# A pre-activation convolution on one core: the half sums m1 and m2 in a tile each

## The chip, the cores and the metric

The kernel runs on one core of a Trainium2 chip. The metric is device time in microseconds (us); the time before is the median of three runs, 1009.18 us (1008.23 to 1009.91). The engines are named as the profile names them: PE (matmuls), PEld (loading of PE's weights), DVE (vector), ACT (scalar), POOL, and SP, which issues transfers.

## The reference

There are 160 images of 128 channels and 32 x 32 pixels, and five weight sets. Each image is normalised in groups of four channels, convolved with the 3 x 3 weights of its set (128 to 128 channels, quantised to two levels first), and the image itself is added.

```python
w = (v1 + v2).reshape(OUT_CH * N, IN_CH, K, K)          # quantised U, N = 5
xb = x.reshape(B // N, N * C, H, W)
act = conv_general_dilated(xb, w, padding=[(1, 1), (1, 1)], feature_group_count=N)
g = v.reshape(B_, 32, C_ // 32, H_, W_)                  # _gn
return ((g - mean(g)) / sqrt(var(g) + 1e-5)).reshape(v.shape)
x = x + conv(_gn(x), U)
```

## The kernel before

Channels lie on the 128 partitions. `Main.run` goes over the 160 images set by set, 32 images for each of five weight sets. The order of the instructions on every engine is written out by hand in that loop, under a manual schedule: nothing is moved by a planner, and each engine works through its own list in order. Waits between engines are set where one engine writes a tile that another reads or overwrites; they go by tile.

**Two precisions.** Every normalised image is split into a float16 part and a float16 remainder, and the product of both with the weights is summed in PSUM. An image is either *direct* or *combined* (L524 to L529): up to image 145 every odd image from 7 on is combined and every even one direct; from image 146 on two of three are combined. For a direct image ACT makes `z` (L513) and `hi` (L521), DVE the remainder `lo` (L579) and its three combinations of rows: the differences (L593), the sums of row pairs (L595) and their differences (L596), all in the tile `rows`. For a combined image POOL and DVE combine the raw image's rows first (`v`: L544, L545, and L555, L558, L561), ACT rounds to `vh` (L566), DVE makes the remainder `vl` (L572).

**The half sums.** The convolution over three rows of taps saves work: for each pair of output rows two half sums are made, m1 and m2, from the sum and the difference of the two input rows, and the pair is m1 + m2 and m1 - m2. They live in the tile `m` (`self.pair`, L380), one PSUM bank for m1 and one for m2. The steps for image i are:

- `sums_of_pairs(i)` (L668, matmuls at L655): PE writes m2's bank first and then m1's. A combined image takes 12 matmuls, 6 for each; a direct one 6, 3 for each. A full one has 512 columns.
- `leave(i)` (L713): ACT copies m2 from PSUM to SBUF.
- `pairs(i)` (L723, L725): DVE writes m1 + m2 and m1 - m2 into the two banks of a tile `eo`, of which there are two. Between the two instructions the caller may put one more step (`between`).
- `rest_of_column(i)` (L619, L655): PE adds the remaining products into `eo`: 24 matmuls of 256 columns for a combined image; 18 of 512 and 12 of 256 for a direct one.
- `residual(i)` (L739): ACT halves `eo` into `sum`, and `accumulate(i)` (L752) adds it to the image with a DMA from POOL's queue. For the first three images and the last four, DVE does this itself (L744). `store` and `load` (L757, L409) are issued on SP.

**The order.** `conv(i)` issues the sums of image i + 1 first and then the rest of image i. In the same iteration DVE makes the remainder of image i + 2, then the pairs of i + 1, then `combine(i + 4)`. ACT does the residual of i - 1, leaves i + 1, and makes the parts of i + 3. Around these ACT takes the statistics of images further ahead: a sum (L192) and a sum of squares (L199) for nearly every image, up to 14 images ahead, until there are no images left, at about iteration 145. Steps that quantise the weights of the next set (the iterator `later`) are strewn between DVE's work. For a direct image i + 2 two of the combinations come before the pairs, and the third comes between the addition and the subtraction:

```python
self.low_part(i + 2)
take(later, 1)
rows = self.combinations(i + 2)
take(rows, 2)
...
self.pairs(i + 1, lambda: take(rows if i % 2 == 0 else later, 1))
run(rows)
```

Image 2, one of the first three, uses the two banks of `m` as its `eo`; L744 reads both in one instruction.

Of the kernel before, what the change touches and what calls it, by code (L numbers as in the profile page):

```python
# [309 lines left out]
class Main:  # L310
# [36 lines left out]
    def __init__(self, tc, ctx, keep, x, u, out):  # L347
        nc = self.nc = tc.nc
        self.imgs, C, self.H, self.W = x.shape
        P = self.P = nc.NUM_PARTITIONS  # L350
        assert C == P and self.H * self.W == 1024
        self.per_set = self.imgs // N_SETS
        self.xv = x.rearrange("(b n) c h w -> n c b (h w)", n=N_SETS)
        self.ov = out.rearrange("(b n) c h w -> n c b (h w)", n=N_SETS)
        self.uv = u.rearrange("n (o i k) -> n o i k", o=C, k=TAPS)

        def pool(name, bufs, **kw):
            return ctx.enter_context(tc.tile_pool(name=name, bufs=bufs, **kw))

        self.const = pool("const", 1)  # L360
        self.qpool = pool("quant", 1)
        self.wpool = pool("weights", 2)
        self.upool = pool("u", 1)
        self.xpool = pool("x", 11)
        self.zpool = pool("z", 3)
        self.parts = pool("parts", 5)
        self.rows = pool("rows", 4)
        self.wide = pool("wide", 2)
        self.wide_parts = pool("wide_parts", 3)
        self.evac = pool("evac", 2)  # L370
        self.sums = pool("sums", 3)
        self.unread = pool("unread", 1)
        self.small = pool("small", 3)
        self.ps_eo = pool("ps_eo", 2, space=PSUM)
        self.ps_m = pool("ps_m", 1, space=PSUM)
        self.ps_stat = pool("ps_stat", 1, space=PSUM)
        self.ps_tr = pool("ps_tr", 1, space=PSUM)
        self.steps = Steps(nc, keep)

        self.pair = self.ps_m.tile([P, 2, self.H // 2, self.W], F32, tag="m", name="m")  # L380
        self.chunks, self.z, self.hi, self.v, self.eo, self.m2 = {}, {}, {}, {}, {}, {}
        self.sum = {}
        self.wts = {}
        self.columns = []

        cuts = [0, 2, 4, 8, 12, 16, 20, *range(24, self.imgs + 1, 8)]
        self.groups = [range(a, b) for a, b in zip(cuts, cuts[1:])]
        self.group_of = {i: k for k, g in enumerate(self.groups) for i in g}
        self.stats = {}
# [215 lines left out]
    def taps(self, i, part, col, target, last, halves=(0, 1)):  # L605


        nc, H, W = self.nc, self.H, self.W
        tile, top = part
        n, _ = self.place(i)  # L610
        dw = col - 1
        c0, c1 = max(0, -dw), W - max(0, dw)
        for k in (1, 0, 2):
            for h in halves:

                h0 = h * (H // 2)
                r0, r1 = max(h0, 1 - k), min(h0 + H // 2, H + 1 - k)
                s0 = r0 + k - 1 + top
                nc.tensor.matmul(  # L619
                    target[:, h, r0 - h0 : r1 - h0, c0:c1],  # L620
                    self.wts[n, col][:, k, :],
                    tile[:, s0 : s0 + r1 - r0, c0 + dw : c1 + dw],
                    start=(i < self.FIRST and col == self.COLS[0] and k == 1 and top == 0),
                    stop=(last and k == 2),
                    skip_group_check=True,
                )

    def bank_pair(self, i):
        return self.ps_eo.tile([self.P, 2, self.H // 2, self.W], F32, tag="eo", name=f"eo{i}")

    def warm_up(self, count):


        zeros = self.los[3].rearrange("p h w -> p (h w)")
        for _ in range(count):
            self.nc.tensor.matmul(
                self.pair[:, 0].rearrange("p i w -> p (i w)"), zeros[:, :128],
                zeros[:, :512], start=True, stop=True,
            )

# [26 lines left out]

    def sums_of_pairs(self, i):  # L668

        m = self.pair  # L670
        both = self.both(i)
        for a, kind in ((1, self.DIFF), (0, self.SUM)):
            for col in self.COLS:
                for j, (_, st) in enumerate(both):
                    self.product(
                        m[:, a], i, kind, st[:, a], col,
                        col == self.COLS[0] and j == 0,
                        col == self.COLS[-1] and j == len(both) - 1,
                    )
# [30 lines left out]
    def leave(self, i):  # L710

        m2 = self.evac.tile([self.P, self.H // 2, self.W], F32, tag="m2", name=f"m2_{i}")
        self.nc.scalar.copy(m2, self.pair[:, 1])  # L713
        self.m2[i] = m2

    def pairs(self, i, between=lambda: None):


        nc = self.nc
        m1, m2 = self.pair[:, 0], self.m2.pop(i)  # L720
        eo = self.eo[i] = self.bank_pair(i)
        rows = eo.rearrange("p h (i a) w -> p (h i) a w", a=2)
        nc.vector.tensor_add(rows[:, :, 0], m1, m2)  # L723
        between()
        nc.vector.tensor_sub(rows[:, :, 1], m1, m2)  # L725
# [5 lines left out]
    def residual(self, i):  # L731

        nc = self.nc
        eo = self.eo.pop(i).rearrange("p h r w -> p (h r w)")
        del self.hi[i]
        n, b = self.place(i)
        if not self.by_hand(i):
            self.sum[i] = self.sums.tile([self.P, 1024], F32, tag="sum", name=f"sum{i}")
            nc.scalar.mul(self.sum[i], eo, 0.5)  # L739
            return  # L740
        xj = self.image(i)
        halves = [slice(0, 512), slice(512, 1024)] if i == self.imgs - 1 else [slice(0, 1024)]
        for h in halves:
            nc.vector.scalar_tensor_tensor(  # L744
                xj[:, h], eo[:, h], 0.5, xj[:, h], ALU.mult, ALU.add
            )
            if i >= self.imgs - LAST:
                nc.sync.dma_start(self.ov[n, :, b, h], xj[:, h])
# [12 lines left out]
    def run(self):  # L761
# [39 lines left out]
        def take(steps, count):  # L801
            for _ in range(count):
                next(steps, None)
# [73 lines left out]
        for i in range(self.imgs):  # L877
# [41 lines left out]
            if i < self.FIRST:  # L919

                if i == 0:
                    measure(0, 8, 9, 10)
                    self.normalise(4)
                    self.high_part(4)
                if i == 2:
                    self.leave(3)
                    self.normalise(5)
                    measure(1, 9)
                    self.high_part(5)
                    self.pairs(3)  # L930
                    self.low_part(4)
                    run(self.combinations(4))
                self.residual(j)
                if i == 1:
                    measure(0, 11)
            else:

                rows = iter(())
                if self.combined(i + 2):
                    self.low_combined(i + 2)  # L940
                elif i + 2 < self.imgs:
                    self.low_part(i + 2)
                    take(later, 1)
                    rows = self.combinations(i + 2)
                    take(rows, 2)
                if i > self.FIRST and self.by_hand(j):
                    self.residual(j)
                for k in by_scalar:
                    self.measure(k, (0,))
                if i > self.FIRST and not self.by_hand(j):  # L950
                    self.residual(j)
                    self.accumulate(j)
                if self.combined(i + 4):
                    self.outer_rows(i + 4)


                part = i + 3 < self.imgs and not self.combined(i + 3)
                if i + 1 < self.imgs:
                    self.leave(i + 1)
                if part:  # L960
                    self.normalise(i + 3)
                    self.high_part(i + 3)
                if self.combined(i + 3):
                    self.high_combined(i + 3)
                for k in by_scalar:
                    self.measure(k, (1,))
# [9 lines left out]
            if i >= self.FIRST:  # L976

                if i + 1 < self.imgs:
                    self.pairs(i + 1, lambda: take(rows if i % 2 == 0 else later, 1))
                run(rows)  # L980
                if self.combined(i + 4):
                    self.combine(i + 4)
                else:
                    take(later, 1)
                if b == self.per_set - 4:
                    run(later)
# [61 lines left out]
```

## Time and profile before

| what | value |
|---|---|
| median of three runs | 1009.18 us (1008.23 to 1009.91) |
| profiled execution, its own time | 1011.2 us |
| its span, first to last instruction | 1009.5 us |
| granted PE clock | 0.999 |
| busy PE, DVE, ACT, POOL | 960.5, 902.2, 912.1, 416.2 us |
| DMA moved | 254.42 MB, 252 GB/s on average |

The first part of the page gives the busy time of each engine as a share of the span. The table of windows gives it by stage, for stretches counted from the start of the span. In a group of instructions the busy time and the mean duration of one stand before the bar, and the time that the engine stood idle just before them behind it, with what ended it. In the list of waits a line names an engine and its line, what it waited for, the total in us, how often, and the longest. In the timeline a line is start, duration, engine, line, operation, what it writes and reads, and in brackets the idle time before it. A matmul's end in the trace is modelled: matmuls that follow one another overlap in the list.

### The profile page before, as it was taken

What the parts mean: (1) busy time and instruction counts of PE and PEld (TensorE: products, weight loads), DVE (VectorE), ACT (ScalarE), POOL (GpSimd) and SP (SyncE); (2) the same over time, 40 slices, a digit from 0 to 9 for tenths busy, and PEclk for the clock granted to TensorE, in tenths of its full rate; (3) what the DMA queues carried; (4) which work ended last, traced back from release to release, by engine and by line L of the source; (5) the groups of instructions that cost most, each with busy time, mean ns of one, the idle gap of its engine ahead of it and who ended that gap; (6) DMA issues with size and microseconds to landing.
All of it is one profiled execution on the core that took longest, in us unless ns stands there. A gap on an engine that the chain in (4) does not pass through costs nothing.

```text
span 1009.5 us, 15999 instructions
## 1 busy us (share of the span) xinstructions
PE 960.5 (95%) x5935; PEld 574.3 (57%) x5935; DVE 902.2 (89%) x1237; ACT 912.1 (90%) x1240; POOL 416.2 (41%) x581
## 2 busy tenths in 40 slices
PE   1999999999999999999999999999999999999996
PEld 0445555565556565665556566655565666655564
DVE  7999999998999999889999998998899988898884
ACT  4879999999999999999999999999999999997560
POOL 3535474553425262523434343427263723234220
PEclk9999999999999999999999999999999999999999
DMA  9529979999999999999999999998999999998664
GB/s 358 199 84 238 254 220 288 265 257 267 264 270 282 271 256 272 269 282 263 271 272 259 275 267 264 271 268 242 266 269 268 249 286 269 264 260 217 167 172 145
DMA packets 67287, 254.42 MB, mean 252 GB/s; under 512 B 5248, under 2 KB 5248, under 8 KB 67200
## 3 DMA queue, kind: packets, MB, share of 16 engines
q1 hardware_dynamic: 45168, 173.09, 50.6%
q0 software_dynamic: 22032, 80.23, 40.8%
q8 instruction: 48, 0.79, 0.3%
q14 instruction: 39, 0.32, 0.1%
HBM read 89.19 MB, written 83.89 MB: 171 GB/s over the span
## 4 chain that ended last, share of the span: by engine, by line
PE 55%; ACT 15%; DVE 11%; issue 6%; DMA 6%; POOL 6%; SPq 0%; POOLq 0%; ACTq 0%; DVEq 0%
PE m L655 19%; PE eo L619 19%; PE eo L655 15%; ACT junk L199 3%; DMA xt<-in_x_dram 3%; ACT vh L566 3%; DMA xt<-sum 2%; ACT m L713 2%; ACT sum L739 2%; DVE eo L723 2%; DVE eo L725 2%; ACT z L513 2%; DVE vl L572 1%; POOL rstd L235 1%; ACT junk L192 1%
## 5 line engine op out<-in xcount | busy, mean ns | idle before, releaser
L655 PEld LDWEIGHTS <-wt 128*128 128x128 f16 x4266 | 413.5, 98 | 255.8 <-DVE eo L725 25.0
L619 PE MATMUL eo<-hi,wt 128*128 128x496 f16 (+3 forms) x1422 | 339.7, 375 | 1.1 <-ACT wt L478 0.6
L752 POOL DMA_DIRECT2D xt<-sum x153 | 136.4, 895 | 425.7 <-ACT sum L739 409.2
L619 PEld LDWEIGHTS <-wt 128*128 128x128 f16 x1494 | 146.1, 99 | 143.0 <-ACT wt L478 1.8
L655 PE MATMUL m<-vh,wt 128*128 128x496 f16 (+1 forms) x480 | 182.7, 381 | 15.2 <-DVE eo L725 14.6
L572 DVE SCALAR_TENSOR_TENSOR vl<-v,rstd,vh 128x2048 f16<-128x2048 f32 x80 | 187.9, 2349 | 4.0 <-ACT vh L566 4.0
L655 PE MATMUL eo<-vh,wt 128*128 128x248 f16 (+1 forms) x960 | 184.0, 273 | 0.0
L655 PE MATMUL eo<-vl,wt 128*128 128x248 f16 (+1 forms) x960 | 184.0, 273 | 0.0
L655 PE MATMUL m<-vl,wt 128*128 128x496 f16 (+1 forms) x480 | 182.3, 380 | 0.0
L723 DVE TENSOR_TENSOR eo<-m,m 128x512 f32<-128x512 f32 x157 | 109.1, 695 | 80.2 <-ACT m L713 80.1
L192 ACT ACTIVATE junk<-xt 128x1024 f16<-128x1024 f32 x152 | 160.6, 1057 | 20.4 <-DMA xt<-in_x_dram 17.4
L199 ACT ACTIVATE junk<-xt,mv 128x1024 f16<-128x1024 f32 x152 | 174.0, 1145 | 0.2
L566 ACT ACTIVATE vh<-v,rstd 128x2048 f16<-128x2048 f32 x80 | 161.0, 2013 | 3.0 <-POOL v L545 2.0
L739 ACT ACTIVATE sum<-eo 128x1024 f32<-128x1024 f32 x153 | 154.0, 1006 | 8.2 <-PE eo L655 7.8
L655 PE MATMUL eo<-rows,wt 128*128 128x256 f16 (+1 forms) x924 | 139.0, 273 | 0.0
L713 ACT COPY m<-m 128x512 f32<-128x512 f32 x157 | 91.1, 580 | 38.9 <-PE m L655 36.2
L655 PE MATMUL m<-rows,wt 128*128 128x496 f16 (+1 forms) x462 | 112.5, 380 | 1.0 <-DVE rows L596 0.8
L725 DVE TENSOR_TENSOR eo<-m,m 128x512 f32<-128x512 f32 x157 | 108.5, 691 | 1.2
L513 ACT ACTIVATE z<-xt,shift,rstd 128x1024 f32<-128x1024 f32 x80 | 99.5, 1244 | 4.0 <-POOL shift L242 4.0
L579 DVE TENSOR_TENSOR lo<-z,hi 128x1024 f16<-128x1024 f32 x80 | 97.8, 1223 | 0.3 <-ACT hi L521 0.3
L555 DVE TENSOR_TENSOR v<-xt 128x960 f32<-128x960 f32 x80 | 91.8, 1147 | 0.0
L521 ACT CAST hi<-z 128x1024 f16<-128x1024 f32 x80 | 83.6, 1046 | 2.5
(111 smaller groups left out, 874.9 us busy)
## 6 DMA issues: line engine op xcount, KB each, us to landing
xt<-in_x_dram SPq DMA_DIRECT2D x78, 1024.0 KB, 8.8
out_dram<-xt SPq DMA_DIRECT2D x78, 1024.0 KB, 5.1
xt<-sum POOLq DMA_DIRECT2D x153, 512.0 KB, 7.1
range<-in_L_conv_U_dram SPq DMA_DIRECT2D x4, 576.0 KB, 8.0
u<-in_L_conv_U_dram SPq DMA_DIRECT2D x4, 576.0 KB, 11.4
xt<-in_x_dram SPq DMA_DIRECT2D x4, 512.0 KB, 10.5
out_dram<-xt SPq DMA_DIRECT2D x3, 512.0 KB, 2.7
u<-in_L_conv_U_dram SPq DMA_DIRECT2D x2, 288.0 KB, 3.1
```

The lines of the kernel that those rows point to most:

```text
L192: self.nc.scalar.activation(junk, image, ACTF.Copy, scale=-1.0 / image.shape[1], accum_out=self.mv[:, j, 0:1],)
L199: self.nc.scalar.activation(junk, image, ACTF.Square, bias=self.mv[:, j, 0:1], accum_out=self.mv[:, j, 1:2],)
L513: nc.scalar.activation(z, self.image(i), ACTF.Identity, bias=st.shift[:, j : j + 1], scale=st.rstd[:, j : j + 1],)
L566: self.nc.scalar.mul(vh, self.v[i], st.rstd[:, j])
L572: self.nc.vector.scalar_tensor_tensor(vl, self.v[i], st.rstd[:, j], self.hi[i], ALU.mult, ALU.subtract)
L619: nc.tensor.matmul(target[:, h, r0 - h0 : r1 - h0, c0:c1], self.wts[n, col][:, k, :], tile[:, s0 : s0 + r1 - r0, c0 + dw : c1 + dw], start ...
L655: self.nc.tensor.matmul(target[:, :, c0:c1], self.wts[n, col][:, kind, :], source[:, :, c0 + dw : c1 + dw], start=start, stop=stop, skip_g ...
L713: self.nc.scalar.copy(m2, self.pair[:, 1])
L723: nc.vector.tensor_add(rows[:, :, 0], m1, m2)
L725: nc.vector.tensor_sub(rows[:, :, 1], m1, m2)
L739: nc.scalar.mul(self.sum[i], eo, 0.5)
L752: self.nc.gpsimd.dma_start(self.image(i), self.sum.pop(i), accum_op=ALU.add)
```

## The change

`m` becomes two tiles, `m1` and `m2`, of one bank each, so that waits for one are no longer waits for the other. All that touched `self.pair[:, a]` now takes `self.pair[a]`; for image 2, whose `eo` the pair is, a helper `bank` picks the half, and its residual is done in two instructions of 512 columns. The three combinations of a direct image all come before the pairs, and only a step of `later`, in odd iterations, is left between the addition and the subtraction. The rule which images are combined (L529) is the same in both kernels. Line numbers below L380 shift by 2 to 12 in the changed kernel.

```diff
-        self.pair = self.ps_m.tile([P, 2, self.H // 2, self.W], F32, tag="m", name="m")
+        self.pair = [
+            ps_m.tile([P, self.H // 2, self.W], F32, tag=name, name=name) for name in ("m1", "m2")
+        ]
...
-                    target[:, h, r0 - h0 : r1 - h0, c0:c1],
+                    self.bank(target, h)[:, r0 - h0 : r1 - h0, c0:c1],
...
+    def bank(self, target, h):
+        return target[h] if target is self.pair else target[:, h]
+
...
     def sums_of_pairs(self, i):
-        m = self.pair
         both = self.both(i)
         for a, kind in ((1, self.DIFF), (0, self.SUM)):
             for col in self.COLS:
                 for j, (_, st) in enumerate(both):
                     self.product(
-                        m[:, a], i, kind, st[:, a], col,
+                        self.pair[a], i, kind, st[:, a], col,
...
-        self.nc.scalar.copy(m2, self.pair[:, 1])
+        self.nc.scalar.copy(m2, self.pair[1])
...
-        m1, m2 = self.pair[:, 0], self.m2.pop(i)
+        m1, m2 = self.pair[0], self.m2.pop(i)
...
-        halves = [slice(0, 512), slice(512, 1024)] if i == self.imgs - 1 else [slice(0, 1024)]
-        for h in halves:
+        if i == self.imgs - 1 or eo is self.pair:
+            parts = [
+                (slice(h * 512, h * 512 + 512), self.bank(eo, h).rearrange("p r w -> p (r w)"))
+                for h in range(2)
+            ]
+        else:
+            parts = [(slice(0, 1024), eo.rearrange("p h r w -> p (h r w)"))]
+        for h, part in parts:
             nc.vector.scalar_tensor_tensor(
-                xj[:, h], eo[:, h], 0.5, xj[:, h], ALU.mult, ALU.add
+                xj[:, h], part, 0.5, xj[:, h], ALU.mult, ALU.add
             )
...
-                rows = iter(())
                 if self.combined(i + 2):
                     self.low_combined(i + 2)
                 elif i + 2 < self.imgs:
                     self.low_part(i + 2)
                     take(later, 1)
-                    rows = self.combinations(i + 2)
-                    take(rows, 2)
+                    run(self.combinations(i + 2))
...
-                    self.pairs(i + 1, lambda: take(rows if i % 2 == 0 else later, 1))
-                run(rows)
+                    self.pairs(i + 1, lambda: take(later, i % 2))
```

More of the change, by code (lines that the diff above doesn't have):

```diff
@@ L374, in __init__ @@
         self.ps_eo = pool("ps_eo", 2, space=PSUM)
-        self.ps_m = pool("ps_m", 1, space=PSUM)
+        ps_m = pool("ps_m", 1, space=PSUM)
         self.ps_stat = pool("ps_stat", 1, space=PSUM)
@@ L636, in warm_up @@
             self.nc.tensor.matmul(
-                self.pair[:, 0].rearrange("p i w -> p (i w)"), zeros[:, :128],
+                self.pair[0].rearrange("p i w -> p (i w)"), zeros[:, :128],
                 zeros[:, :512], start=True, stop=True,
@@ L733, in residual @@
         nc = self.nc
-        eo = self.eo.pop(i).rearrange("p h r w -> p (h r w)")
+        eo = self.eo.pop(i)
         del self.hi[i]
@@ L738, in residual @@
             self.sum[i] = self.sums.tile([self.P, 1024], F32, tag="sum", name=f"sum{i}")
-            nc.scalar.mul(self.sum[i], eo, 0.5)
+            nc.scalar.mul(self.sum[i], eo.rearrange("p h r w -> p (h r w)"), 0.5)
             return
         xj = self.image(i)
-        halves = [slice(0, 512), slice(512, 1024)] if i == self.imgs - 1 else [slice(0, 1024)]
-        for h in halves:
+        if i == self.imgs - 1 or eo is self.pair:
[6 more added lines that the diff above has]
+        for h, part in parts:
             nc.vector.scalar_tensor_tensor(
-                xj[:, h], eo[:, h], 0.5, xj[:, h], ALU.mult, ALU.add
+                xj[:, h], part, 0.5, xj[:, h], ALU.mult, ALU.add
             )
```

## The prediction

> **What bounds the kernel now.** The page's first part comes first: PE, ACT and DVE are all near 90%, so no share names a bound. It is read by stage, in the table of windows.
>
> ```profile
> PE 960.5 (95%) x5935; PEld 574.3 (57%) x5935; DVE 902.2 (89%) x1237; ACT 912.1 (90%) x1240; POOL 416.2 (41%) x581
> ```
>
> ```profile
> 60.00:240.00 180.00, 174.78 (x1076) 103.27 (x1074) 171.03 (x248) 169.38 (x237) 94.32 (x116) 1.00 0.89 243
> 240.00:812.00 572.00, 567.56 (x3540) 341.88 (x3539) 521.87 (x704) 559.37 (x763) 238.74 (x324) 1.00 0.99 267
> 812.00:912.00 100.00, 100.00 (x619) 59.98 (x617) 86.79 (x106) 98.05 (x132) 30.86 (x51) 1.00 1.00 270
> 912.00:1001.00 89.00, 81.68 (x530) 51.06 (x529) 71.03 (x80) 47.37 (x50) 25.20 (x36) 1.00 0.65 173
> ```
>
> After the span come window, length, then PE, PEld, DVE, ACT, POOL busy, clock, DMA share, GB/s. From 240 to 912 us PE and ACT are both at 98% or more; after 912 us ACT has no statistics left (53% busy), yet PE idles 7.3 us of 89. The list of waits says what PE idles for, first for 60 to 912 us, then for 912 to 1001 us (total, times, longest).
>
> ```profile
> DVE eo L723 <- ACT m L713: 66.4, 72, 1.7
> PEld L655 <- DVE eo L725: 16.3, 34, 1.5
> PE m L655 <- DVE eo L725: 7.5, 13, 1.2
> ACT m L713 <- PE m L655: 6.4, 17, 2.9
> ACT junk L192 <- DMA xt<-in_x_dram: 5.6, 6, 1.6
> ACT sum L739 <- PE eo L655: 0.8, 2, 0.4
> ```
> ```profile
> ACT m L713 <- PE m L655: 29.9, 14, 7.1
> DVE eo L723 <- ACT m L713: 13.7, 8, 2.7
> PEld L655 <- DVE eo L725: 8.7, 5, 2.1
> PE m L655 <- DVE eo L725: 7.3, 5, 1.8
> ```
>
> It is a ring: PE's sums wait for DVE's subtraction (L725), DVE for ACT's copy (L713), ACT for PE's sums. The timeline shows one turn of it.
>
> ```profile
> 508.79 1.46 PE L655 MATMUL m<-rows,wt 128*128 128x512 f16 x6
> 510.55 0.57 ACT L713 COPY m<-m 128x512 f32<-128x512 f32 x1
> 511.16 0.70 DVE L723 TENSOR_TENSOR eo<-m,m 128x512 f32<-128x512 f32 x1 [1.08 <-ACT m L713]
> 512.31 0.68 DVE L725 TENSOR_TENSOR eo<-m,m 128x512 f32<-128x512 f32 x1
> 513.05 0.39 PE L655 MATMUL m<-vh,wt 128*128 128x512 f16 x1 [0.17 <-DVE eo L725]
> ```
>
> A 512-column matmul starts every 0.217 us though it is shown 0.38 us long, so a PE gap is understated by 0.16 us. True loss to L725: 7.5 + 34 × 0.16 = 13.0 us before 912, and 7.3 + 5 × 0.16 = 8.1 us after: 21.1 us. Nearly all of these gaps stand before the twelve sums of a combined image (`m<-vh`) that follow a direct one's six: between lie only the 24 half-width matmuls of a combined image, 24 × 0.108 = 2.6 us, in which copy, addition, the step between and subtraction (0.6 + 0.6 + 0.55 + 0.7 = 2.5 us) have to fit.
>
> **What the Trainium skill says.** "PSUM — Partial Sum Buffer", "PSUM bank collisions raise a hardware error": engines must be kept apart by bank, and in different banks run side by side. Here copies of m2 (L713) take 572 to 601 ns throughout, though PE writes eo's banks during most. Its "Engine vs sequencer instructions": ACT and DVE are strict queues and matmuls keep their order; the timeline agrees, every row stands in the order of the code. "Perfetto Trace Analysis", "Tensor Engine Instruction (MATMUL, LD_WEIGHTS)": a matmul's end is estimated, which is the 0.38 against 0.217 us above. Its "Identifying Dependency Chains": an instruction that waits for two engines may get an event-semaphore instruction in front. The trace has 152 of these before L739, which starts 92 ns after the start of the accumulator read, as L217 and L231 do without one: no visible price.
>
> **The change, part by part.** In the built streams the waits differ as follows.
>
> (1) ACT's copy waits for m2's matmuls alone, 3 or 6 of 0.217 us (0.65 or 1.3 us) earlier. (2) PE's m2 group waits for that copy, no longer for L725; the m1 group waits for L725. So L725 may end 1.3 us later (six matmuls of a combined image) before PE stops. Queued behind that new wait: the m1 sums and all later matmuls of PE; L723, L739 and the next copy wait for those. The copy ends at least 1.4 us (L723 + L725) before L725 does, so the wait at m1 stays the one that decides. (3) L723 now waits for PE's m1 too: 157 event semaphores on DVE, 0 to 30 ns each (the gap that ACT shows before L192, which has one), at most 4.7 us beside 80 us of DVE waiting: 0. Where the copy starts at once, m1's end (0.65 us after m2's) and the copy's (0.6) coincide.
>
> (4) The third combination (L596, 413 ns, some 0.35 us start to start) moves ahead of L723 for direct images. It delays L723 there, not L725, which comes sooner where DVE had to wait for the copy; PE takes those m sums 1.3 us or more after L725, and DVE waits beside it. 0. No DMA moves and ACT, POOL and SP issue the same in the same order. (5) Image 2's residual becomes two 512-wide instructions (0.685 each against 1.216 us): +0.15 us at 54 us on DVE; I take 0.2, bounds 0 to 0.5. The addresses of the banks and the rule which images are combined (L529) stay, so "every second image combined" costs nothing: it's not in the diff.
>
> What is regained, by stage:
>
> 912 to 1001 us. The period of three images is 18.75 to 18.89 us. PE needs 2 × 24 + 30 = 78 matmuls' worth, 16.9 us; DVE 2 × (2.34 combine + 2.28 vl) + 2.6 (lo and rows) + 3 × 1.4 = 16.0 us. Placing 149's sums: PE reaches them 2.2 us earlier (its 1.86 stall and the 0.39 one before); m1 comes 1.3 later; L725 of 148 ends 0.65 earlier, as DVE's chain started from a copy that waited for PE. Left: about 0.3 us of stall, likewise in the next period, then less. Gain 8.1 - 0.5 = **7.6 us**, bounds 5 (L725 no earlier: 4 × 0.56 + 0.39 = 2.6 stay, and 13 event semaphores of 30 ns are added) and 8.1.
>
> 60 to 912 us. Stalls are at most 1.2 + 0.16 us, so PE alone would regain nearly all 13.0. But ACT, in its fixed order, is not waiting: from 240 to 812 us it is busy 559.4 of 572 us. What it waits for PE is all it can give back: 6.4 + 0.8, less 2.2 of one 2.9 us wait that gets only 0.65 shorter, plus waits under 150 ns that the list leaves out (27 before the copies, together 2.7 us). **7.7 us**, of which 3.4 before 240 us. Bounds: 3 (DMA takes the middle part) and 13.0 (ACT's other gaps close too). What is late next is ACT, whose copy then makes PE wait for it.
>
> Sum: 7.6 + 7.7 - 0.2 = 15.1 us. The profiled execution took 1011.2 us, span 1009.5 plus 1.7 around it; it would take 996.1. The median, 1009.18, is 2.0 below the profiled one: 994.1.
>
> **Rivals.** PE sets the pace: all 21.1 us less 0.2, 988.3. For it: PE is at its matmul rate from 812 to 912 us, without a stall, while ACT keeps up (98.05 busy). Against it: before 812 ACT also scales three columns of weights for each set.
>
> The DMA ring sets it: a load is issued behind a store that waits for an accumulating DMA, and the loads land 0.1 to 4 us before ACT's L192 needs them; DMA share is 0.99 to 1.00. From 812 to 912 us, at an unstalled 11.73 us for two images, ACT waited for loads twice, 1.1 us in all. If faster running only uses up this slack, 240 to 912 us gives nothing: and 3.4 + 7.6 - 0.2 = 10.8 us are left: 998.4, or with more waits for loads 1001.
>
> No change: m1 and m2 tracked apart in name only, or the stalls reappear one for one at m1 because ACT's copy is late by the same: within 2 us. The built waits and (2) speak against it.
>
> Slower: the new waits cost PE itself. The built PE stream has 155 more rows with a wait, now in mid-stream between the m2 and m1 groups. If a satisfied wait let the array run empty (0.16 us, the tail of a matmul), 155 × 0.16 = 24.8 us against 15.1: 1019. It decides from 15.1 / 155 = 0.097 us each. Against it: where a matmul waits today for ACT with the copy long done, it starts 0.217 us after its predecessor.
>
> **How the numbers follow.** A measurement of this kernel tells about 0.2% (2 us) from no change. ACT sets the pace 0.58 (990 to 999), the DMA ring 0.18, PE 0.14, no change 0.05, slower 0.05. Faster 0.90, same 0.05, slower 0.05. The predicted time is the first case's, 994.1. The range takes in most of the first three: 989 to 1001.
>
> **What would show it.** Right: waits of L655 for L725 nearly gone after 912 us and small before; periods of three images near 17 us there; ACT L713's waits for PE gone from 100 to 900 us; ACT busy 99% and PE waiting for L713 or L725 at m1 in single places. L192's waits for DMA rising from 5.6 us to 10 or more would show the DMA ring. Wrong: the spacing from the last m2 to the first m1 matmul above 0.25 us everywhere (slower), or a PE loss to L725 above 10 us.

## The result, and the profile after

The changed kernel takes 996.24 us, the median of four runs (993.94 to 998.77), against 1009.54 us (1008.23 to 1010.14): a ratio of 0.9871, with a 95% interval of 0.9844 to 0.9897. (Here and below, medians and spreads are of all executions, ratios only of those within 1.5% of the fastest of the same kernel.) The prediction was 994.1 us, with a range of 989 to 1001. The profiled execution is the slowest of the four, 998.77 us, with a span of 997.1 us; it lies 12.4 us below the profiled execution of before.

In the changed kernel the copy of m2 is L717 (L713 before), the addition L727 (L723), the subtraction L729 (L725), the matmuls of the sums L660 (L655), the residual L743 (L739). First the engines' busy time and three groups from the page, and below them the first of these groups on the page of before.

```profile
PE 959.2 (96%) x5935; PEld 578.0 (58%) x5935; DVE 910.4 (91%) x1238; ACT 907.4 (91%) x1240; POOL 427.0 (43%) x581
...
L660 PE MATMUL m<-vh,wt 128*128 128x496 f16 (+1 forms) x480 | 182.2, 380 | 2.4 <-DVE eo L729 1.4
...
L727 DVE TENSOR_TENSOR eo<-m,m 128x512 f32<-128x512 f32 x157 | 109.0, 694 | 57.6 <-ACT m L717 50.3
...
L717 ACT COPY m<-m 128x512 f32<-128x512 f32 x157 | 90.8, 579 | 13.8 <-PE m L660 13.8
```
```profile
L655 PE MATMUL m<-vh,wt 128*128 128x496 f16 (+1 forms) x480 | 182.7, 381 | 15.2 <-DVE eo L725 14.6
```

The work is the same; PE and ACT are busy within 5 us of before, while DVE shows 8 us more and POOL 11 us more. PE's idle time just before a combined image's sums was 15.2 us and is 2.4 us. The windows by stage follow, with the same columns as before.

```profile
240.00:812.00 572.00, 567.28 (x3539) 343.96 (x3537) 528.41 (x706) 556.42 (x765) 251.08 (x325) 1.00 0.99 269
812.00:912.00 100.00, 100.00 (x623) 60.66 (x622) 85.13 (x100) 98.44 (x132) 31.60 (x54) 1.00 0.98 266
912.00:989.00 77.00, 76.74 (x506) 49.20 (x505) 68.52 (x79) 42.22 (x43) 22.73 (x33) 1.00 0.69 185
```

From 912 to 989 us PE is busy 76.74 us of 77, where it had been idle 7.3 us of 89. Between 240 and 812 us it is as busy as before, 567.3 against 567.6 us. The starts of PE's sums in the timeline show where the 12.4 us come from:

| PE's sums of image | before, us | after, us | gain of the stage, us |
|---|---|---|---|
| 3 | 56.67 | 56.00 | 0.67 |
| 33 | 240.59 | 236.02 | 3.90 |
| 129 | 811.63 | 807.08 | -0.02 |
| 146 | 913.25 | 908.48 | 0.22 |
| end of the span | 1009.5 | 997.1 | 7.6 |

The first 0.67 us isn't counted as a gain of the change: that start lies between 54.7 and 57.0 us over the profiled executions of all the kernels below, whatever their code.

The same two images as in the turn of the ring shown before the change, now in the timeline of the changed kernel (both tiles are listed as `m`):

```profile
504.03 1.46 PE L660 MATMUL m<-rows,wt 128*128 128x512 f16 x6
506.01 0.57 ACT L717 COPY m<-m 128x512 f32<-128x512 f32 x1
506.62 0.70 DVE L727 TENSOR_TENSOR eo<-m,m 128x512 f32<-128x512 f32 x1 [0.67 <-ACT m L717]
507.75 0.69 DVE L729 TENSOR_TENSOR eo<-m,m 128x512 f32<-128x512 f32 x1
507.96 0.38 PE L660 MATMUL m<-vh,wt 128*128 128x512 f16 x1
...
509.25 0.38 PE L660 MATMUL m<-vh,wt 128*128 128x512 f16 x1
```

PE starts m2 at 507.96 us, while the subtraction that still reads m1 runs until 508.44; m1 starts at 509.25, six matmuls later, without a wait. ACT's copy starts 1.98 us after the first of the direct image's sums, and it isn't PE that it waits for: no idle time is noted behind it. It is late because ACT is at work.

The list of waits, first from 60 to 907 us, then from 907 to 989 us:

```profile
DVE eo L727 <- ACT m L717: 50.3, 58, 1.6
...
ACT junk L192 <- DMA xt<-in_x_dram: 11.2, 8, 3.9
...
PE pg L225 <- POOL dv L222: 3.2, 6, 1.1
...
ACT m L717 <- PE m L660: 2.2, 1, 2.2
...
PE m L660 <- DVE eo L729: 1.8, 5, 0.6
```
```profile
ACT sum L743 <- PE eo L660: 18.2, 10, 3.8
ACT m L717 <- PE m L660: 11.6, 10, 7.1
DVE eo L727 <- PE m L660: 7.0, 5, 2.7
```

ACT's waits for PE before its copy, 6.4 us in 17 places before, are one wait of 2.2 us now, that of image 4. ACT's waits for loads of images doubled, from 5.6 to 11.2 us. A wait has grown that was 0.3 us there: that of PE's statistics matmul (L225) for POOL's `dv`, a step of the statistics, since PE now runs further ahead of ACT, from which `dv` comes.

### The profile page after: what moved, and what is told of

It is laid out like the page before. It is cut to its first block, busy times and chain, and to the rows that moved or that the text cites. A ratio compares the mean times of both kernels' runs of the same rounds, so it can differ in the third digit from the quotient of the medians.

```text
span 997.1 us, 16155 instructions
## 1 busy us (share of the span) xinstructions
PE 959.2 (96%) x5935; PEld 578.0 (58%) x5935; DVE 910.4 (91%) x1238; ACT 907.4 (91%) x1240; POOL 427.0 (43%) x581
## 4 chain that ended last, share of the span: by engine, by line
ACT 27%; PE 24%; DVE 18%; DMA 11%; issue 10%; POOL 8%; SPq 0%; ACTq 0%; POOLq 0%; DVEq 0%
PE m L660 8%; PE eo L660 8%; PE eo L621 8%; ACT vh L568 7%; DMA xt<-in_x_dram 7%; ACT sum L743 7%; ACT junk L199 6%; DMA xt<-sum 4%; ACT m L717 4%; DVE v L557 3%; DVE eo L727 2%; DVE eo L729 2%; DVE v L560 2%; DVE v L563 2%; ACT junk L192 2%
## 5 line engine op out<-in xcount | busy, mean ns | idle before, releaser
L660 PEld LDWEIGHTS <-wt 128*128 128x128 f16 x4266 | 417.3, 98 | 235.8 <-issue 7.2
L660 PE MATMUL m<-vh,wt 128*128 128x496 f16 (+1 forms) x480 | 182.2, 380 | 2.4 <-DVE eo L729 1.4
L660 PE MATMUL eo<-vh,wt 128*128 128x248 f16 (+1 forms) x960 | 183.9, 273 | 0.0
L660 PE MATMUL eo<-vl,wt 128*128 128x248 f16 (+1 forms) x960 | 183.9, 273 | 0.0
L660 PE MATMUL m<-vl,wt 128*128 128x496 f16 (+1 forms) x480 | 182.2, 380 | 0.2 <-DVE vl L574 0.2
L743 ACT ACTIVATE sum<-eo 128x1024 f32<-128x1024 f32 x153 | 154.3, 1009 | 19.8 <-PE eo L660 19.4
L727 DVE TENSOR_TENSOR eo<-m,m 128x512 f32<-128x512 f32 x157 | 109.0, 694 | 57.6 <-ACT m L717 50.3
L660 PE MATMUL eo<-rows,wt 128*128 128x256 f16 (+1 forms) x924 | 138.9, 273 | 0.0
L660 PE MATMUL m<-rows,wt 128*128 128x496 f16 (+1 forms) x462 | 113.0, 380 | 0.7 <-DVE eo L729 0.4
L729 DVE TENSOR_TENSOR eo<-m,m 128x512 f32<-128x512 f32 x157 | 109.3, 696 | 3.6
L717 ACT COPY m<-m 128x512 f32<-128x512 f32 x157 | 90.8, 579 | 13.8 <-PE m L660 13.8
```

Source lines behind the costliest of these rows:

```text
L660: self.nc.tensor.matmul(target[:, :, c0:c1], self.wts[n, col][:, kind, :], source[:, :, c0 + dw : c1 + dw], start=start, stop=stop, skip_g ...
L717: self.nc.scalar.copy(m2, self.pair[1])
L743: nc.scalar.mul(self.sum[i], eo.rearrange("p h r w -> p (h r w)"), 0.5)
```

## The experiments

Ratios are to runs of the kernel before on the same chip, with 95% intervals. Line numbers of the variants can differ by a few from those of the changed kernel.

**The two tiles alone** (`split_only`): the third combination goes back between the addition and the subtraction.

```diff
+                rows = iter(())
...
-                    run(self.combinations(i + 2))
+                    rows = self.combinations(i + 2)
+                    take(rows, 2)
...
-                    self.pairs(i + 1, lambda: take(later, i % 2))
+                    self.pairs(i + 1, lambda: take(rows if i % 2 == 0 else later, 1))
+                run(rows)
```

> The two tiles alone, with the third combination back between the addition and the subtraction. Theory A (the wait of PE's m2 sums for the subtraction was the loss, and the split takes it away): all of the gain stays, 995 to 998 us, and waits of PE for the subtraction stay below 4 us. Theory B (the gain comes from the subtraction that no longer stands behind a combination): most of it goes, 1005 to 1009 us.

Measured: 996.55 us, ratio 0.9874 (0.9847 to 0.9901). The whole gain is there. In its profiled execution (995.59 us) the stage from image 33 to 129 took 565.46 us, against 571.04 before and 571.06 in the profiled execution of the changed kernel; from 240 to 800 us ACT's waits for loads were 6.8 us in it, and 11.2 us in the other (from 60 to 912 us 9.9 and 11.2):

```profile
ACT junk L192 <- DMA xt<-in_x_dram: 6.8, 7, 1.6
```

**The combinations in front alone** (`comb_only`), in the kernel before:

```diff
-                rows = iter(())
...
-                    rows = self.combinations(i + 2)
-                    take(rows, 2)
+                    run(self.combinations(i + 2))
...
-                    self.pairs(i + 1, lambda: take(rows if i % 2 == 0 else later, 1))
-                run(rows)
+                    self.pairs(i + 1, lambda: take(later, i % 2))
```

> The combinations in front of the pairs alone, m1 and m2 in one tile as before. Theory A: no gain, 1007.5 to 1010.5 us; the 18 waits of PE for the subtraction (14.8 us before) stay within 2 us of that, since nearly all of them stand behind a direct image's pairs, where a step of the weights and not a combination lies between. Theory B: 996 to 1003 us.

Measured: 1009.44 us (14 executions, one of them 1704.2 us), ratio 0.9995 (0.9984 to 1.0006): nothing. PE's waits for the subtraction are what they were, in this list of waits:

```profile
PEld L655 <- DVE eo L725: 24.8, 37, 2.0
PE m L655 <- DVE eo L725: 15.1, 18, 1.7
```

With these two, the gain is the split's, and the moved combination is free.

**The other half first** (`m1_first`): two tiles, but m1 is written before m2.

```diff
-        for a, kind in ((1, self.DIFF), (0, self.SUM)):
+        for a, kind in ((0, self.SUM), (1, self.DIFF)):
```

> The changed kernel, but PE writes m1's sums before m2's. ACT's copy then waits for all the sums again, and PE's first matmul of a group waits for the subtraction as it did before. Theory A (what counts is that six m2 matmuls stand ahead of the wait): the gain goes, 1007 to 1011 us, PE again idles some 20 us for the subtraction. Rival C (two tiles are enough, in either order, since finer waits let each engine go on sooner): 995 to 1000 us.

Measured: 1009.24 us, ratio 0.9998 (0.9985 to 1.0010). The gain is gone although the tiles are apart, and both of the old waits are back:

```profile
ACT m L717 <- PE m L660: 35.7, 28, 7.1
PEld L660 <- DVE eo L729: 20.7, 33, 1.8
PE m L660 <- DVE eo L729: 14.9, 18, 1.7
```

So what pays is not the finer wait as such. It is the order: the half whose release comes early (m2, by the copy) is written first, so that it covers the wait for the half whose release comes late (m1, by the subtraction). The rival that two tiles are enough in any order falls. The edit takes back both steps of the prediction at once, the earlier copy (1) and the wait that six matmuls cover (2); how the gain divides between these two is not shown.

**Loads of images two images earlier** (`lead20_after`):

```diff
-    LOAD_LEAD = 18
+    LOAD_LEAD = 20
```

> The changed kernel with LOAD_LEAD 20 for 18: each load of images is issued two images earlier, behind the store that has just been issued and into the place that this store empties. It is a test of what holds the stretch from 240 to 812 us, in which the profile after gains nothing. If it is the ring of the transfers (ACT waits 11.2 us for loads): these waits fall below 3 us and the time falls by 3 to 8 us, to 988 to 993 us. If ACT's own work holds it: waits for loads fall and PE waits in their place, 994 to 998 us. If the store that the load now waits for is too late: more waits for loads, over 998 us.

Measured: a median of 1014.71 us; its executions spread from 997.0 to 1022.9 us, apart from one far longer, so that the ratio (0.9969, 0.9945 to 0.9994, from 8 of the 22) says little. In its profiled execution (1016.72 us) ACT's waits for loads fell to 1.8 us from 60 us on, but something else was late:

```profile
DVE nn L99 <- DMA u<-in_L_conv_U_dram: 25.2, 3, 13.1
```

The weights' load stands in SP's queue behind a load that waits for a store. This execution is one of the long ones; whether the weights were late in the short ones too is not shown. So the two edits were made together, with the weights' load moved two images ahead.

**Earlier loads and earlier weights**, in the changed kernel (`lead20_set`) and in the kernel before (`lead20_set_before`):

```diff
-    LOAD_LEAD = 18
+    LOAD_LEAD = 20
...
-                if b == (2 if n == 0 else 0):
-                    self.load_set(n + 1)
+                if n == 0 and b == 2:
+                    self.load_set(n + 1)
+                if b == self.per_set - 2 and n + 2 < N_SETS:
+                    self.load_set(n + 2)
```

> The changed kernel with LOAD_LEAD 20, and with the next set's weights loaded two images earlier (issued at the 31st image of the set before). With LOAD_LEAD 20 alone, ACT no longer waited for images, but DVE waited 25.2 us in three places for the weights, whose load stood in SP's queue behind a load that waits for a store. If the transfers' ring is what held the stretch from 240 to 812 us after the change: both waits are gone and the time is 987 to 992 us. If ACT's own work holds it: 993 to 997 us with PE waiting for ACT and DVE instead.

> The same two edits of the loads in the kernel before, with m1 and m2 in one tile. If the ring of PE, ACT and DVE held the kernel before, earlier loads bring little: 1005 to 1010 us, with waits for loads below 2 us after the start and PE's idle time for the subtraction still 13 us or more. If the transfers' ring alone had held it: 996 to 1002 us.

Measured: 1020.38 us, ratio 1.0117 (1.0089 to 1.0145), and 1019.08 us, ratio 1.0105 (1.0064 to 1.0145). Both missed: they are slower than with the loads at their old place. In the changed kernel the weights are no longer late, but ACT waits for images more than ever, in 31 places from 60 us on:

```profile
ACT junk L192 <- DMA xt<-in_x_dram: 35.8, 31, 3.7
```

In this execution SP waits 675 us in all for stores to land before it issues loads; in the changed kernel it waits 812 us for the accumulating transfers, and for no store. The loads asked for earlier come later here: from image 33 to 129 a load is issued 0.4 us (median) before PE starts the sums of the image 14 places back, against 5.0 us in the changed kernel. As a test of the transfers these runs fail, since they take the waits away in no version. They show only what late loads cost the changed kernel: from image 33 to 129 ACT waits 18.2 us longer for them, and the stage takes 16.8 us longer.

**Less work on ACT** (`act_less`), in the changed kernel, and the same with the earlier loads (`act_less_lead20_set`). Both leave a part of the statistics out, the squares of most columns of every second image:

```diff
+        if self.short and j % 2:
+            junk, image = junk[:, :64], image[:, :64]
         self.nc.scalar.activation(
             junk, image, ACTF.Square, bias=self.mv[:, j, 0:1],
...
+        st.short = i >= 32
```

> The changed kernel, with ACT's sum of squares (L199) taken over 64 of 1024 columns for every second image from image 32 on: it leaves that part of the statistics out, some 0.8 us of ACT per two images, 50 us in all. If ACT's work held the stretch from 240 to 812 us: PE's matmuls set the pace, 986 to 990 us. If the transfers held it: ACT waits for loads that much longer (40 us or more) and the time stays at 993 to 998 us.

> Both: earlier loads of images and weights, and the squares over 64 columns for every second image from image 32 on (that part of the statistics is left out). Neither ACT nor the transfers are then in the way, so PE's matmuls set the pace: 984 to 989 us, PE idle below 2 us from 240 us on. If it stays at the time of the earlier loads alone, within 1.5 us, ACT's work was no bound there.

Measured: 991.48 us, ratio 0.9837 (0.9815 to 0.9858), and 1022.60 us, ratio 1.0103 (1.0059 to 1.0147). In the second ACT waits 67.6 us for loads from 60 us on, so that its relief buys nothing: with the loads that late, they hold the kernel. The first lies between the two ranges expected (986 to 990 and 993 to 998), and its stages decide between ACT and the transfers. The window from 240 to 800 us of the changed kernel and, below it, that of `act_less`, then ACT's waits in the latter:

```profile
240.00:800.00 560.00, 555.28 (x3466) 336.75 (x3464) 518.09 (x693) 544.51 (x750) 247.37 (x319) 1.00 0.99 269
240.00:800.00 560.00, 560.00 (x3512) 341.33 (x3510) 523.96 (x698) 518.10 (x761) 236.08 (x323) 1.00 1.00 273
```
```profile
ACT sum L747 <- PE eo L664: 24.7, 35, 0.9
ACT junk L193 <- DMA xt<-in_x_dram: 13.7, 10, 3.1
```

PE has no gap left in 560 us: images 33 to 129 take 563.72 us, 7.3 less than in the changed kernel. The transfers keep up with PE's pace, at a share of 1.00. ACT waits 13.7 us for loads here too, and it costs nothing, because ACT now has time to wait. In the changed kernel as it is ACT has hardly any (555.5 of 571.1 us busy from image 33 to 129, and 11.2 of the other 15.6 us are waits for loads), so each wait for a load is added to its stream.

**More statistics on DVE**, a change that keeps the computation: five (`vec5`: 50, 66, 82, 98, 114), eleven (`vec11`: every eighth image from 42 to 122), eleven in the kernel before (`vec11_before`), and nine (`vec9`: every eighth from 58 to 122, the diff shown).

```diff
-    BY_VECTOR = (8, 10, 11, 14, 19, 24, 29, 34)
+    BY_VECTOR = (8, 10, 11, 14, 19, 24, 29, 34, 58, 66, 74, 82, 90, 98, 106, 114, 122)
```

> The changed kernel with the statistics of five more images (50, 66, 82, 98, 114) made by DVE instead of ACT: some 2.3 us off ACT for each and 1.9 us on DVE, which waits there for ACT's copies anyway. If ACT's stream, with its waits for loads, is what holds the stretch from 240 to 812 us after the change: part of that stretch's loss is regained, 992 to 995 us. If DVE is as near its bound as ACT: 996 us or more.

Measured: 995.34 us, ratio 0.9845 (0.9820 to 0.9869): above the range expected if ACT's stream was the bound, and not told from the changed kernel by its interval. In its profiled execution images 33 to 129 take 566.92 us.

> The same with eleven more images (every eighth, 42 to 122): ACT loses some 26 us, DVE gains 20 us. If ACT's stream holds that stretch: PE's matmuls set the pace there and the time is that with the shortened squares or a little above, 990.5 to 993.5 us. If DVE becomes the bound: PE's waits for the subtraction come back, 996 us or more.

Measured: 995.65 us, ratio 0.9857 (0.9834 to 0.9880): a miss in the total. By stage, images 33 to 129 take 563.79 us, as with the shortened squares: PE's pace was reached. But images 3 to 33 take 182.26 us against 180.02, where PE waited 1.3 us for DVE's `vl` just after image 42 had been measured.

> The kernel before with the same eleven images measured by DVE. If the ring of PE, ACT and DVE through the one tile m held it before: relief of ACT alone regains little, and less than in the changed kernel, 1004 to 1010 us; the last stretch, from 912 us, keeps its 8 us of PE's idle time. If ACT's work alone was the bound before: 1001 us or less.

Measured: 1014.64 us, ratio 1.0038 (1.0023 to 1.0054): slower, outside what either theory gave. PE's waits for the subtraction rose:

```profile
PEld L655 <- DVE eo L725: 28.7, 41, 2.6
PE m L655 <- DVE eo L725: 18.1, 21, 2.4
```

Some 3 us of this are lost before image 33, as 2 us are with the two tiles. From image 33 to 129 the same edit makes the one-tile kernel 1.8 us slower (572.87 us, against 569.9 to 571.0 in the four kernels with the old waits and the old statistics) and the two-tile kernel 7.3 us faster. In the one-tile kernel DVE is a link of the ring that stops PE, so work put on DVE lengthens the ring, whatever it takes off ACT. This is the clearest sign that before the change the ring and not ACT's load was the bound.

> The changed kernel with nine more images on DVE (every eighth from 58 to 122), without 42 and 50. With eleven, PE waited 1.4 us for DVE's vl at 226 us, just behind the extra statistics of image 42, while the stretch from 240 to 812 us ran at PE's rate (0.4 us lost). If ACT's stream is what held that stretch: 992 to 994.5 us, 1 to 3 us below the eleven. If the statistics on DVE cost as much elsewhere as they save: 995 to 997 us, as the changed kernel.

Measured: a median of 993.33 us, ratio 0.9858 (0.9826 to 0.9890). Its median is in the range expected and 2.9 us below the changed kernel's, and images 33 to 129 take 564.95 us; but the intervals of the ratios overlap, so it's not shown to be faster. From 240 to 800 us:

```profile
240.00:800.00 560.00, 559.50 (x3506) 340.69 (x3504) 535.03 (x742) 532.45 (x721) 247.71 (x323) 1.00 1.01 273
```

ACT is 12 us less busy than in the changed kernel's same window, DVE 17 us more.

## Why the prediction was right, and where not

**The ring and its loosening** (1, 2): right. m2's sums wait for the copy, m1's for the subtraction, and six matmuls lie between; `m1_first` shows that their order counts.

**The last stage**: 7.6 us predicted, 7.6 measured; that the two agree to a tenth is luck. The two stalls that the placing of the sums left in part, 0.3 us each, came out as 0.6 us once (at image 149, 0.3 of it for `vl`, which the prediction didn't name), and none in the later periods, which take 16.9 us, PE's own time.

**60 to 240 us**: 3.4 predicted, 3.9 measured (from image 3 to 33).

**240 to 912 us**: 4.3 predicted, -0.02 + 0.22 = 0.2 measured in the profiled execution. The step that failed here is "What it waits for PE is all it can give back", in two sizes. ACT gave back more than its idle time: between images 33 and 129 the gaps before its copies fell from 3.9 us to 0, and a copy that doesn't wait starts some 0.1 us before the end of the instruction ahead of it, which saved 3.1 us more (this overlap grew from 6.7 to 9.8 us in 96 copies). That is 7.0 us. But ACT's waits for loads, whose growth the main case put at nothing, rose by 6.7 us and took it all. In the profiled execution of `split_only` the loads took 2.2 us, and the stage gained 5.6 us. So the main case's 4.3 us lies between two executions, and the 2.1 us by which the median lies above the forecast (996.24 against 994.1) are of the size of this spread. That the total came so near is in part luck.

The rival "The DMA ring sets it" thus has a part: in the profiled execution its sign (waits of 10 us or more) and its gain of nothing for this stage came true, by way of ACT. In `split_only` the waits were 9.9 us from 60 to 912 us, 6.8 of them from 240 to 800, and the stage from image 33 to 129 gained 5.6 us all the same. As a bound of its own it fell: with ACT relieved, PE ran gapless at about the same transfer share. That transfers are late in some executions and not in others isn't explained.

**What I costed at nothing**: the moved combination is free (`comb_only`). The 157 event semaphores of L727 are there, and where DVE doesn't wait it starts 336 ns (median) after the start of the last combination, as the same addition (L723) does in `comb_only`, which has no such semaphores: no price. The two-instruction residual of image 2 can't be seen in the scatter of the start of image 3's sums.

**The rivals**: PE setting the pace (988.3) was refuted for the changed kernel, since ACT is late; even with ACT relieved the median is 991.48. The slower case, an emptied array at 155 new waits, did not come: in 148 of 160 images the first m1 matmul starts 0.217 us or less after the last of m2. "No change" fell with the result.

**What was not foreseen**: PE running ahead of ACT arrives early at the statistics matmuls and waits 3.2 us for `dv` from 60 to 907 us, the largest single kind of PE's gaps there after the change. One of them:

```profile
353.64 0.39 PE L225 MATMUL pg<-dv,gavg 128*128 128x8 f32 x2 [1.07 <-POOL dv L222]
```

## What to carry to other kernels

Where one buffer of two banks is emptied by two engines one after the other, give each bank a tile of its own, and write first the bank that is released first: the work on it covers the release of the second. Then ask who is late next; here it was the engine that had hardly been idle all along, and in one of two executions its waits for transfers took back what it had gained. Work moved onto an engine that is a link of the ring can make a kernel slower even if the engine seems to have time: here DVE, at 89% before.

## What the runs showed of the hardware

A second semaphore for 157 vector instructions cost nothing that can be seen (336 ns start to start, with and without). A copy on ACT that had nothing to wait for started 97 to 126 ns before the end of the instruction ahead of it, so that a wait costs ACT more than the idle time shown. With loads that queue behind the store of their own slot (`lead20_set`, in which the weights' loads move too) the kernel took 1020.38 us against 996.24, though they stand two images earlier in the program.
